# Rotary tables on GpSimd, latent masks as planned steps, a later second norm and a first copy on ScalarE in a three-part transformer kernel

## The chip, the cores and the metric

The kernel runs on one core of one Trainium2 chip. The metric is the device time of one launch in microseconds. A core has five engines with a queue each: TensorE (PE in the profile, its weight loads PEld), VectorE (DVE), ScalarE (ACT), GpSimd (POOL) and SyncE (SP), which here only issues DMAs. Each queue is worked off in the order in which the program put its instructions. An instruction that waits for another engine holds up what is queued behind it.

## The reference

The input x has 8 sequences of 512 tokens with 128 channels. Three blocks follow one another: a feed-forward stack at half weight, a causal attention with low-rank (latent) projections, and the same feed-forward stack again.

```
x = x + 0.5 * ffn(layernorm(x))
x = x + latent_attention(layernorm(x))     # 16 heads of 8, causal
x = x + 0.5 * ffn(layernorm(x))

ffn(x), for each of two layers l:
  h = shift_token(x)                       # half the channels come from the token before
  q, k, v = split(h @ wqkv[l])             # 8 heads of 64
  q = l2norm(q) * q_scale[l]; k = l2norm(k) * k_scale[l]
  q, k = rotary_xpos(q, k)
  x = x + local_attention(8 * q, k, v) @ wo[l]          # window of 64, one window back
  h = layernorm(shift_token(x)) * ln_g[l] + ln_b[l]
  a, g = split(h @ w1[l] + b1[l])
  x = x + (a * gelu(g)) @ w2[l] + b2[l]
```

All arithmetic is in float32, but for masks in bfloat16 that are added by products.

## The kernel before, in words

The program has three parts: `ffn("f0")`, `latent_attention()` and `ffn("f1")`. A feed-forward part goes over two layers and eight sequences (l, b), each sequence in four blocks of 128 tokens. A block is projected to q, k and v on TensorE (L542). ScalarE squares q and k (L568). DVE multiplies them by the rotary tables (c at L552, s at L555), GpSimd adds the two (L576) and later scales k (L612). Transposes (L504), scores (L675), a maximum on DVE (L684, L685), exponentials on ScalarE (L692), a division on GpSimd (L700), transposes of the probabilities, products with v (L758) and the output projection (L782) follow. After the fourth block comes the sequence's gated feed-forward (L849 to L902).

**The planner.** In the two `ffn` parts nobody writes the order of the instructions by hand. The code registers steps with a kind, an engine, a cost in microseconds and a rank, together with what they read and write. The rank is 100 times a position k (four per sequence, one per block) plus a number per kind from the table `PLACE`. `Plan.run` (L159 on) then keeps a clock for each engine. Again and again it takes the engine on which a step can begin first, and of its steps that can begin by then, the one of lowest rank. Only the first 110 steps by rank are looked at (`AHEAD`, L89). The order found so is fixed: it is the order of each queue on the chip. A change of one cost or rank can therefore reorder what comes after it.

**The head of the program.** Before the plan of f0, the code at L285 to L335 makes constants on GpSimd: the identity, two `band` masks for the local attention, and then three masks of the latent attention (`rows_of`, `causal`, `causal_t`; memsets at L317, selects at L325) and two rows of constants, `rows_sb` (L332). These stand ahead of all planned steps in GpSimd's queue, since they are not steps. The masks are first read by the masked products of the latent maxima (L1288), which the planner places near the end of f0; `rows_sb` is read by `fill_rows`, a DMA on SP.

**A sequence's beginning.** `shift(l, b, k)` begins a sequence. In layer 0 it has a norm in four steps: statistics on DVE (L484 to L486, kind "ist"), a logarithm and an exponential on ScalarE (L467, L468, "inr"), one Newton step on GpSimd (L471 to L474, "inn"), and the application on DVE (L492, "ina"). Then TensorE transposes ("sh"), and two copies fill hT: the first half of the channels on DVE (L520, "sd") and the half shifted by a token on ScalarE (L528, "sa").

**The rotary tables.** `rotary_table(l, s, ...)` (L344 on) multiplies the constant table by q_scale or k_scale of one layer. It is called four times (two layers, q and k), each time with three products, as steps of kind "tb" with rank `100 * 2 * l - 450`. Their inputs lie in the buffer `u` of the feed-forward. The latent weights use it next (loads at L984, products at L998, copies at L1004), and afterwards the feed-forward itself.

Of the kernel before, what the change touches and what calls it, by code (L numbers as in the profile page):

```python
# [16 lines left out]
P = 128  # L17
# [12 lines left out]
    "hs": 650, "hd": 390, "he": 330, "fst": 40, "fnr": -330, "fnn": 790, "fna": -289, "b2": 60,  # L30
    "ft": 620, "fc": 750, "g": 1010, "ge": 950, "a": 1, "u": 161, "po": 1030, "y2": 870,
    "ld": -1100, "lst": -900, "lnr": -880, "lnn": -870, "lna": -860, "lz": -1000, "lo": -990, "l3": -300, "l4": -290, "lt": -850, "lx": -840, "lq": -830, "lc": -820, "ls": -810, "lv": -700, "lu": -690, "lm": -600, "lr": -590, "lf": -400, "et": 0, "ed": 0, "ex": 0, "ev": 0, "es": 0, "ep": 0, "ee": 0,
    "lw": -400, "tb": -450, "fi": 990, "fo": 1230,
}


# [152 lines left out]
def kernel(  # L189
# [121 lines left out]
    def quadrant(g):  # L311
        return slice(32 * g, 32 * g + 32)

    masks = {}
    for name in ("rows_of", "causal", "causal_t"):
        masks[name] = const.tile([P, 4, P], BF16, name=name)
        nc.gpsimd.memset(masks[name], 0.0)  # L317
    for g in range(4):
        for name, pattern, sign, op, fill in (
            ("rows_of", [[-32, 4], [1, P]], -1, ALU.not_equal, 1.0),  # L320
            ("causal", [[32, 4], [-1, P]], 1, ALU.is_ge, MASKED),
            ("causal_t", [[-32, 4], [1, P]], -1, ALU.is_ge, MASKED),
        ):
            rows = masks[name][quadrant(g)]
            nc.gpsimd.affine_select(  # L325
                out=rows, in_=rows, pattern=pattern, compare_op=op, fill=fill, base=0,
                channel_multiplier=sign,
            )

    rows_sb = const.tile([4, 2, P], F32, name="rows_sb")  # L330
    for k in range(2):
        nc.gpsimd.memset(rows_sb[:, k], float(k))  # L332

    def fill_rows(dst, k):
        nc.sync.dma_start(  # L335
# [7 lines left out]

    def rotary_table(l, s, rot_sb, scales):  # L344
        t, g = tabs[l], scales[:, s, l]
        nc.vector.tensor_mul(
            t[:, 2 * s], rot_sb[:, 2 * s], g.unsqueeze(1).to_broadcast([P, NB, DH])
        )
        for lo, fr in ((0, HD), (HD, 0)):
            nc.vector.tensor_mul(  # L350
                t[:, 2 * s + 1, :, lo : lo + HD],
                rot_sb[:, 2 * s + 1, :, lo : lo + HD],
                g[:, fr : fr + HD].unsqueeze(1).to_broadcast([P, NB, HD]),
            )
# [53 lines left out]
    def ffn(tagname, last):  # L408
        plan = Plan(tc, nc)

        def step(kind, engine, cost, at, *args, **kw):
            return plan.step(kind, engine, cost, 100 * at + PLACE[kind], *args, **kw)
# [95 lines left out]
        def shift(l, b, k):  # L508

            y = [("Y", b, i) for i in range(NB)]  # L510
            if l == 0:
                norm(k, "i", lambda: X[:, b], lambda: Y[:, b], [("X", b)], y, [])
            tp, hT = Slot(mm), Slot(r_hT)
            half = C // 2
            step(
                "sh", PE, 0.5, k, lambda: transposes(lambda i: Y[:, b, i], tp),
                y + ([("W", l)] if l else []), [tp], [tp], 0.1,
            )
            step(
                "sd", DVE, 0.62, k, lambda: nc.vector.tensor_copy(hT[:half, :], tp[:half, :]),  # L520
                [tp], [(hT, 0)], [tp, hT], 0.1,
            )
            step(
                "sp", POOL, 0.1, k, lambda: nc.gpsimd.memset(hT[half:, 0:1], 0.0),
                [], [(hT, 1)], [hT],
            )
            step(
                "sa", ACT, 0.5, k, lambda: nc.scalar.copy(hT[half:, 1:T], tp[half:, 0 : T - 1]),  # L528
                [tp], [(hT, 2)], [tp, hT], 0.1,
            )  # L530
            seqs[l, b] = hT, Slot(r_kT), Slot(r_V2), Slot(r_V)
# [395 lines left out]
        def first_loads():  # L927

            tables_u = Slot(r_u)
            size = 4 * NB * DH  # L930

            def rotary():
                return flat(tables_u.tile)[:, :size].rearrange(
                    "p (f n d) -> p f n d", f=4, n=NB
                )

            def scales():
                return flat(tables_u.tile)[:, size : size + 2 * L * DH].rearrange(
                    "p (s l d) -> p s l d", s=2, l=L
                )  # L940

            for t, scale in enumerate((q_scale, k_scale)):
                load_step(
                    0, lambda t=t, scale=scale: nc.sync.dma_start(
                        out=scales()[:, t].rearrange("p l d -> p (l d)"),
                        in_=scale.rearrange("l d -> (l d)").partition_broadcast(P),
                    ), [tables_u], [tables_u],
                )
            load_step(0, lambda: nc.sync.dma_start(out=rotary(), in_=rot), [tables_u], [tables_u])
            for l in range(L):  # L950
                for t in range(2):
                    step(
                        "tb", DVE, 1.2, 2 * l,
                        lambda l=l, t=t: rotary_table(l, t, rotary(), scales()),
                        [tables_u], [("tab", l, t)], [tables_u],
                    )
            load_step(0, lambda: nc.sync.dma_start(out=cols_sb, in_=cols), [("W", 0)])
            for what in load_layer(0):
                load_step(1, what, [("W", 0)])
            for b in range(1, B):  # L960
                load_step(NB * b, lambda b=b: load_tokens(b), [("X", b)])
            load_step(
                NB * 3, lambda: nc.sync.dma_start(out=wqkv_sb[1], in_=wqkv[1]), [("W", 1)]
            )
            for what in load_layer(1):
                load_step(NB * 4, what, [("W", 1)])
            latent_weights()

        def latent_weights():

# [38 lines left out]
        def latent_begins():  # L1009
# [4 lines left out]
            for b in range(2):  # L1014
                q, kk, v = Slot(r_kT), Slot(r_V), Slot(r_V2)
                for name, t in (("q", q), ("k", kk), ("v", v)):
                    head_slots[name, b] = t
                    step(
                        "lz", POOL, 1.95, k, lambda t=t: nc.gpsimd.memset(t.tile, 0.0),
                        [], [t], [t], 0.0, [done[L - 1, B - 2 + b, NB - 1], done[L - 1, B - 1, 0]],  # L1020
                    )
                step("lo", SP, 0.55, k, lambda kk=kk: fill_rows(kk.tile, 1), [kk], [kk], [kk], 1.8)
                step(
                    "lz", POOL, 0.3, k,
                    lambda b=b: nc.gpsimd.memset(heads("v", b)[:, :, :, MD : MD + 1], 1.0),
                    [v], [v], [v],
                )
# [49 lines left out]
            for b, held in [(0, held) for held in MAXIMA] + [(1, held) for held in MAXIMA[:LEAD]]:  # L1077
                q, kk = head_slots["q", b], head_slots["k", b]
                m = maxima_of(b)
                for half in (0, 1):  # L1080
# [6 lines left out]
                        lambda b=b, held=held, units=units: by_turns(  # L1087
                            [maximum_products(b, held, g, bank) for g, bank in units]
                        ),
                        [(q, "d"), (kk, "d")], banks, [q, kk] + banks, 0.1,  # L1090
                    )
                    for (g, bank), t in zip(units, banks):
                        step(
# [530 lines left out]
```

## Time and profile before

| what | value |
|---|---|
| median of 3 runs | 1869.26 us (1868.18 to 1870.35) |
| the profiled execution, its own time | 1873.94 us |
| its span, first to last instruction | 1872.2 us |
| mean granted TensorE clock | 0.978 |
| first transposes on TensorE | 15.70 us |
| first projection on TensorE (L542) | 18.37 us |
| first gates of a feed-forward (table load before L855) | 138.9 us |
| first masked product of the latent maxima (L1288) | 773.9 us |
| first hT copy of the second half (L520) | 1133.17 us |

Times in the profile are microseconds from the first instruction. A timeline row gives start, duration, engine, line, operation and tiles. A bracket behind it names the idle time before the instruction and what ended that time. A row marked xN stands for N instructions in a row; then the duration is the stretch from the first start to the last end. In the rows of busy time by stretch, each engine's busy microseconds come with the number of its instructions, followed by the clock that TensorE was granted (1.00 is full) and the share of the time that the DMA engines were busy. The page's slices divide the span into 40 parts of 46.8 us; a digit is a share in tenths.

### The profile page before, as it was taken

How to read it: one execution, taken by the hardware profiler on the slowest of the kernel's cores; microseconds unless marked ns; L12 is line 12 of the kernel's file. 1: busy time of each engine (PE TensorE's matmuls, PEld its weight loads, DVE VectorE, ACT ScalarE, POOL GpSimd, SP SyncE). 2: the span in 40 equal slices, each digit the busy share in tenths (PEclk: the TensorE clock that was granted, in tenths of full speed). 3: DMA queues.
4: the chain of work that ended last, by engine and by line, in shares of the span. 5: the costliest groups of instructions: out<-in, count | busy, mean ns of one | idle time of the engine just before them, and what ended most of it. 6: DMA issues, size and time to landing. Idle time of an engine off the chain costs nothing.

```text
span 1872.2 us, 50913 instructions
## 1 busy us (share of the span) xinstructions
PE 1751.0 (94%) x19860; PEld 1178.7 (63%) x19860; DVE 1371.9 (73%) x2884; ACT 1391.0 (74%) x3911; POOL 988.0 (53%) x1685
## 2 busy tenths in 40 slices
PE   4999999999999999899999998999999999999998
PEld 2656666666666656477777764666666666666665
DVE  5878877777778777567767646878877777777764
ACT  2888888878888877227667666878888888788875
POOL 5776666666666666100000015867666666666651
PEclk8999999999999999769999999999999999999999
DMA  3211111111111111100000000111111111111110
GB/s 100 51 38 31 30 24 24 24 24 25 26 24 24 24 24 25 29 3 26 16 16 16 15 3 18 27 24 24 30 24 24 24 29 24 30 31 34 30 32 23
DMA packets 51968, 50.03 MB, mean 27 GB/s; under 512 B 22759, under 2 KB 34705, under 8 KB 51729
## 3 DMA queue, kind: packets, MB, share of 16 engines
q1 hardware_dynamic: 51584, 46.00, 10.6%
q8 instruction: 158, 2.59, 0.6%
q10 hardware_dynamic: 144, 0.79, 0.1%
q14 instruction: 82, 0.66, 0.1%
HBM read 6.30 MB, written 2.10 MB: 4 GB/s over the span
## 4 chain that ended last, share of the span: by engine, by line
PE 57%; DVE 18%; ACT 13%; POOL 7%; issue 4%; DMA 1%; SPq 1%; ACTq 0%; DVEq 0%; POOLq 0%
PE mm_f L542 10%; PE mm_f L504 8%; PE mm_f L849 6%; ACT pr_f L692 5%; PE mm_f L782 4%; PE st L1355 4%; PE sc L1297 4%; PE mm_f L891 4%; PE mm_f L758 4%; PE lo L1372 3%; DVE c_f L552 3%; DVE s_f L555 3%; PE sc_f L675 3%; ACT sq_f L568 3%; PE mm_f L1297 2%
## 5 line engine op out<-in xcount | busy, mean ns | idle before, releaser
L692 ACT ACTIVATE pr_f<-sc_f,nm_f,q_f 128x128 f32<-128x128 f32 x1024 | 458.0, 473 | 6.0 <-DVE nm_f L685 4.7
L542 PE MATMUL mm_f<-wqkv,hT_f 128*128 128x512 f32 x768 | 396.4, 621 | 30.8 <-DVE s_f L555 13.8
L576 POOL TENSOR_TENSOR qk_f<-c_f,s_f 128x512 f32<-128x512 f32 x256 | 324.7, 1273 | 118.8 <-DVE s_f L555 114.5
L700 POOL TENSOR_TENSOR pr_f<-pr_f,rso_f 128x512 f32<-128x512 f32 x256 | 265.8, 1039 | 219.1 <-DVE rso_f L716 185.0
L552 DVE TENSOR_TENSOR c_f<-mm_f,tab 128x512 f32<-128x512 f32 x256 | 175.1, 684 | 79.5 <-PE mm_f L542 35.1
L692 ACT ACTIVATION_READ_ACCUMULATOR pr_f<-sc_f,nm_f,q_f 128x1 f32 x1024 | 224.9, 220 | 0.0
L568 ACT ACTIVATE sq_f<-mm_f 128x512 f32<-128x512 f32 x256 | 153.3, 607 | 89.6 <-DVE s_f L555 60.8
L1366 ACT ACTIVATE pl<-st 128x512 f32<-128x512 f32 x280 | 156.2, 596 | 64.0 <-PE st L1355 54.8
L849 PE MATMUL mm_f<-fT_f,w 128*128 128x512 f32 (+1 forms) x384 | 191.7, 615 | 9.0 <-ACT ge_f L855 7.0
L504 PEld LDWEIGHTS mm_f<-ident,qk_f 128*128 128x128 f32 x1024 | 114.9, 142 | 125.3 <-POOL qk_f L612 49.7
L542 PEld LDWEIGHTS mm_f<-wqkv,hT_f 128*128 128x128 f32 x768 | 126.6, 195 | 103.0 <-issue 43.3
L684 DVE TENSOR_REDUCE nm_f<-sc_f 128x8 f32<-128x1024 f32 x128 | 155.2, 1213 | 45.2 <-PE sc_f L675 45.1
L504 PE MATMUL mm_f<-ident,qk_f 128*128 128x128 f32 x1024 | 160.3, 281 | 28.1 <-POOL qk_f L612 11.8
L758 PEld LDWEIGHTS mm_f<-pT_f,V_f 128*64 128x64 f32 (+1 forms) x4096 | 147.4, 136 | 60.2 <-issue 15.3
L758 PE MATMUL mm_f<-pT_f,V_f 128*64 128x64 f32 (+1 forms) x4096 | 179.8, 230 | 0.7 <-ACT pT_f L738 0.7
L555 DVE TENSOR_TENSOR s_f<-mm_f,tab 128x512 f32<-128x512 f32 x256 | 173.8, 679 | 0.0
L1387 POOL TENSOR_TENSOR X<-X,lon 128x128 f32<-128x128 f32 x27 | 11.9, 456 | 299.7 <-DVE lon L1381 299.4
L504 PE MATMUL mm_f<-ident,pr_f 128*128 128x128 f32 x1024 | 155.9, 279 | 11.8 <-DVE u_f L880 3.0
L504 PEld LDWEIGHTS mm_f<-ident,pr_f 128*128 128x128 f32 x1024 | 116.1, 142 | 74.5 <-POOL pr_f L700 32.7
L600 DVE TENSOR_REDUCE rn_f<-sq_f 128x16 f32<-128x1024 f32 x128 | 153.6, 1200 | 7.4 <-ACT sq_f L568 7.4
L782 PEld LDWEIGHTS mm_f<-wo,oT_f 128*128 128x128 f32 x1024 | 127.7, 191 | 43.1 <-ACT oT_f L771 18.2
L782 PE MATMUL mm_f<-wo,oT_f 128*128 128x128 f32 x1024 | 140.7, 280 | 3.3 <-ACT oT_f L771 2.9
(166 smaller groups left out, 3861.1 us busy)
## 6 DMA issues: line engine op xcount, KB each, us to landing
V_f<-V_f SPq DMA_DIRECT2D x224, 128.0 KB
hs_f<-Y SPq DMA_DIRECT2D x32, 112.0 KB
X<-in_x_dram SPq DMA_DIRECT2D x8, 256.0 KB
out_dram<-hs_f SPq DMA_DIRECT2D x8, 256.0 KB
Y<-fl SPq DMA_DIRECT2D x32, 32.0 KB
kT_f<-fl SPq DMA_DIRECT2D x32, 32.0 KB
V_f<-fl SPq DMA_DIRECT2D x32, 32.0 KB
wqkv<-in_wqkv_dram ACTq DMA_DIRECT2D x1, 768.0 KB
```

Of the source, the lines that this page charges most:

```text
L504: nc.tensor.transpose(dst[:, i * P : (i + 1) * P], src(i), ident)
L542: nc.tensor.matmul(ps.tile, lhsT=hT[:, i * P : (i + 1) * P], rhs=wqkv_sb[l][:, at * INNER : (at + 1) * INNER], start=True, stop=True,)
L552: nc.vector.tensor_mul(c1.tile, psv, tabs[l][:, 2 * s, i].unsqueeze(1).to_broadcast([P, H, DH]))
L555: nc.vector.tensor_mul(s1.tile.rearrange("p h (t d) -> p h t d", t=2), psv.rearrange("p h (t d) -> p h t d", t=2)[:, :, ::-1], tabs[l][:, ...
L568: lambda s=s, ps=ps: nc.scalar.activation(sq[:, s], ps.tile, AF.Square),
L576: lambda s=s, c1=c1, s1=s1: nc.gpsimd.tensor_add(qk[:, s].rearrange("p (h d) -> p h d", d=DH), c1.tile, s1.tile),
L692: nc.scalar.activation(pr[:, h], sv[:, h % 2, h // 2], AF.Exp, bias=nm[:, h % 2, h // 2 : h // 2 + 1], scale=q8[:, h : h + 1], accum_out=s ...
L700: nc.gpsimd.tensor_mul(pr[:, heads], pr[:, heads], inv[:, heads].unsqueeze(2).to_broadcast([P, H // 2, P]),)
L758: nc.tensor.matmul(o[r * DH : (r + 1) * DH, u * P + w * WIN : u * P + (w + 1) * WIN], lhsT=(V2, V)[w][keys, i, h * DH : (h + 1) * DH], rhs ...
L782: nc.tensor.matmul(pw[:, :C], lhsT=oT[:, pr], rhs=wo_sb[l][:, pr], start=(pr == 0), stop=(pr == INNER // P - 1),)
L849: nc.tensor.matmul(ps[: hsz[c], :], lhsT=w1_sb[l][:, at + c * P : at + c * P + hsz[c]], rhs=fT.tile, start=True, stop=True,)
L1366: nc.scalar.activation(dst, bank, AF.Exp, scale=MSCALE)
```

## The change

It has five edits.

1. The masks and rows at the head become a generator, `mask_parts`. Each of its 17 instructions is a step of its own on GpSimd: kind "lb", cost 0.65, position 5, so rank 500. The steps that read them get "masks" among their reads.
2. `rotary_table` uses GpSimd in place of DVE. Its steps are on POOL with cost 1.3, and their position is 4l in place of 2l.
3. The norm of sequence 1 in layer 0 gets position k + 2 in place of k, so 200 more in rank. That holds in f0 and in f1.
4. The copy "sd" of sequence 0 in layer 0 is done by ScalarE in place of DVE, with the planner's cost left at 0.62. That too holds in both halves.
5. `PLACE` gets an entry for "lb".

```
-    masks = {}
-    for name in ("rows_of", "causal", "causal_t"):
-        masks[name] = const.tile([P, 4, P], BF16, name=name)
-        nc.gpsimd.memset(masks[name], 0.0)
-    for g in range(4):
-        for name, pattern, sign, op, fill in (
...
+    def mask_parts():
+
+        for name, pattern, sign, op, fill in MASKS:
+            yield lambda name=name: nc.gpsimd.memset(masks[name], 0.0)
+            for g in range(4):
+                rows = masks[name][quadrant(g)]
+                yield lambda rows=rows, pattern=pattern, sign=sign, op=op, fill=fill: (
+                    nc.gpsimd.affine_select(
...
+        for k in range(2):
+            yield lambda k=k: nc.gpsimd.memset(rows_sb[:, k], float(k))
...
-        nc.vector.tensor_mul(
+        nc.gpsimd.tensor_mul(
             t[:, 2 * s], rot_sb[:, 2 * s], g.unsqueeze(1).to_broadcast([P, NB, DH])
         )
         for lo, fr in ((0, HD), (HD, 0)):
-            nc.vector.tensor_mul(
+            nc.gpsimd.tensor_mul(
...
             if l == 0:
-                norm(k, "i", lambda: X[:, b], lambda: Y[:, b], [("X", b)], y, [])
+
+                at = k + 2 if b == 1 else k
+                norm(at, "i", lambda: X[:, b], lambda: Y[:, b], [("X", b)], y, [])
...
             step(
-                "sd", DVE, 0.62, k, lambda: nc.vector.tensor_copy(hT[:half, :], tp[:half, :]),
+                "sd", DVE if l or b else ACT, 0.62, k,
+                lambda: (nc.vector.tensor_copy if l or b else nc.scalar.copy)(
+                    hT[:half, :], tp[:half, :]
+                ),
                 [tp], [(hT, 0)], [tp, hT], 0.1,
             )
...
-                        "tb", DVE, 1.2, 2 * l,
-                        lambda l=l, t=t: rotary_table(l, t, rotary(), scales()),
+                        "tb", POOL, 1.3, 4 * l,
+                        lambda l=l, t=t: rotary_table(
+                            l, t, rotary(), scales()
+                        ),
...
             latent_weights()
+            for what in mask_parts():
+                step("lb", POOL, 0.65, 5, what, [], ["masks"])
...
-                step("lo", SP, 0.55, k, lambda kk=kk: fill_rows(kk.tile, 1), [kk], [kk], [kk], 1.8)
+                step(
+                    "lo", SP, 0.55, k, lambda kk=kk: fill_rows(kk.tile, 1), [kk, "masks"], [kk],
+                    [kk], 1.8,
+                )
...
-                        [(q, "d"), (kk, "d")], banks, [q, kk] + banks, 0.1,
+                        [(q, "d"), (kk, "d"), "masks"], banks, [q, kk] + banks, 0.1,
```

## The prediction

> **What bounds the kernel now.** I read the page first, for the engine shares and the slices, since the edits touch a few microseconds of a 1872 us program and the question is whether their stage is bound by something else.
>
> ```profile
> PE 1751.0 (94%) x19860; PEld 1178.7 (63%) x19860; DVE 1371.9 (73%) x2884; ACT 1391.0 (74%) x3911; POOL 988.0 (53%) x1685
> ...
> PE   4999999999999999899999998999999999999998
> ...
> POOL 5776666666666666100000015867666666666651
> ```
>
> TensorE is the bound (94%) everywhere but in the first slice of 46.8 us, where its digit is 4. Time saved in that slice moves all later TensorE work forward, because little after it waits for anything but TensorE. So I took the first stretch apart in the timeline (start, duration, engine, line, operation):
>
> ```profile
> 4.68 0.52 POOL L317 MEMSET rows_of<- 128x512 bf16 x1
> ...
> 8.30 0.20 ACT L468 ACTIVATE ns_f<-ns_f 128x4 f32<-128x4 f32 x1
> ...
> 12.92 0.63 POOL L325 TENSOR_SCALAR_AFFINE_SELECT causal_t<-causal_t 32x512 bf16<-32x512 bf16 x1
> 13.61 0.34 POOL L332 MEMSET rows_sb<- 4x128 f32 x2
> 14.00 0.14 POOL L524 MEMSET hT_f<- 64x1 f32 x2
> 14.22 0.20 POOL L471 TENSOR_TENSOR nt_f<-ns_f 128x4 f32<-128x4 f32 x1
> ...
> 15.29 1.12 DVE L492 TENSOR_SCALAR Y<-X,mv_f,ns_f 128x128 f32<-128x128 f32 x4 [7.27 <-POOL ns_f L474]
> 15.69 0.95 PEld L504 LDWEIGHTS mm_f<-ident,Y 128*128 128x128 f32 x4 [15.69 <-DVE Y L492]
> ```
>
> The input of the first norm's Newton step (L471) is ready at 8.50, when ScalarE ends L468. GpSimd reaches that step only at 14.22, after the mask instructions from 4.68 to 13.95. DVE idles 7.27 us for it, and TensorE starts at 15.69. The DMA answer for 0 to 6 us shows the queue of the first weights finished (0.26 MB up to 3, 0.53 MB from 3 to 6; the tensor has 768 KB), so weights don't hold an earlier start.
>
> Then busy time by stretch (us, then PE, PEld, DVE, ACT, POOL, granted clock, DMA share, GB/s):
>
> ```profile
> 16.00:35.00 19.00, 13.01 (x26) 5.52 (x26) 14.67 (x39) 4.54 (x9) 7.26 (x9) 0.90 0.01 5
> 35.00:55.00 20.00, 16.48 (x115) 8.62 (x115) 16.92 (x37) 11.63 (x38) 13.03 (x25) 0.75 0.18 41
> 55.00:80.00 25.00, 23.73 (x253) 15.80 (x251) 20.45 (x45) 21.49 (x74) 18.16 (x33) 0.93 0.23 62
> ...
> 90.00:112.00 22.00, 20.48 (x237) 13.66 (x235) 17.70 (x38) 17.80 (x58) 18.16 (x38) 1.00 0.22 50
> ```
>
> From 16 to 55 TensorE lacks 9.5 us of work; from 25 to 40 DVE is busy 13.9 of 15 us, so there DVE leads. From 55 on TensorE is 95% busy. GpSimd has its fullest stretch at 90 to 112.
>
> **The change, part by part.** The sum is made against the profiled execution: span 1872.2, its own time 1873.94; the runs' median, 1869.26, is 4.7 lower, and I subtract the same amount from it.
>
> *Masks out of the head.* 17 instructions (3 memsets of 0.52, 12 selects of 0.63, 2 row memsets) leave GpSimd's queue ahead of the Newton step. That step then starts when L468's result arrives, 8.58 (a later pair in the trace, 27.86+0.20 to 28.14, shows 0.08 between them), not at 14.22: **-5.6 us**. X lands at 6.1 in either case, so no more is to be had here.
>
> *Rotary tables on GpSimd.* Each of four steps is three products of two SBUF operands: on DVE 0.42+0.49, 0.9 us. GpSimd's nearest rows are L612 and L700, 128x512 in 1.04: half that size twice over gives 1.04, some 1.2 with three starts. The Trainium skill (GPSIMD Engine Reference, "Engine selection") speaks against the move: such elementwise work belongs on VectorE, GpSimd being about twice as slow. By that rule four steps are 4 x 1.8 = 7.3 us, by the row 4.8. The rotary input should have landed by 9 to 10 (q1 had moved 0.90 MB at 9.0; inputs up to it are 0.93 MB). From 9.6 the first table ends at 10.8 by the row, 11.4 by the rule; all four at 14.4 or 16.9. Their cover is the transposes, the copies of hT and the first projection: the first reader (L552) ran at 21.08 and would be at 15.5, and GpSimd's first add (L576) at 16.8. By the row nothing is exposed; by the rule 0.1 us. I take the row: 0. Without that cover, a late input for instance, each microsecond stalls GpSimd's queue and the projection of q behind it.
>
> The same page's "Key points" warn that GpSimd shares its SBUF interfaces with VectorE. Here the trace has a price: the four L492 of sequence 0 took 1.12 us with GpSimd idle; those of sequence 1 ran beside L576:
>
> ```profile
> 29.13 2.49 POOL L576 TENSOR_TENSOR qk_f<-c_f,s_f 128x512 f32<-128x512 f32 x2
> ...
> 29.90 2.31 DVE L492 TENSOR_SCALAR Y<-X,mv_f,ns_f 128x128 f32<-128x128 f32 x4
> ```
>
> The moved products will run just when sequence 0's L492 do (9.65 to 10.8). Free of contention that is 0, fully contended 2.31-1.12 = 1.2. The products are shorter than the add, so I take half: **+0.6**.
>
> Off DVE: three of the four tables ran in idle time at 16 to 20. The fourth stood at 33.34 in the DVE-led stretch: between 0 and 0.9, I take **-0.7**. The latent weights wait for the tables' buffer, so their seven loads may be issued some 15 us sooner than 34.18. SP had nothing queued then but the second wqkv, and waits for nothing there.
>
> *Second norm further back.* Statistics (25.70 to 27.59) and L492 (29.90 to 32.21) take 4.2 us of DVE's time while projections of sequence 0 wait for it. They are postponed, not removed, and TensorE's projections of sequence 1, its filler at 33.5, come later with them. Between -4.2 (DVE later has 15% slack in the TensorE-bound part) and +3 (filler missing for as long as TensorE idled at 27.0 to 30.1). I take **-1.5**. In the second half these steps run at 1104 to 1107 with DVE mostly idle: 0 there; if they slid into 1135 to 1160, 3.0 us of DVE time would stand in a DVE-led stretch.
>
> *First copy on ScalarE.* Both copies of hT already run one after the other (16.98+0.58, then 17.59+0.68); 0.58 for 0.68 and no change of engine: -0.1. In the second half 0.68 us leaves DVE at 1133. ScalarE has nothing queued behind at the start; in the second half exponentials follow it. From -0.8 to +0.6: **-0.3** in all.
>
> *Masks as steps.* Some 9.8 us of GpSimd work come back with rank 500. The plan looks 110 steps ahead; by my count about 270 steps have a lower rank (37 for each of the first four blocks, parts of the next, loads, latent weights), so the masks appear after about 160, that is around 60 to 110 us. GpSimd is 73% busy there (18.16 of 25), 83% at 90 to 112. A step caught behind one waits up to 0.63 us, and TensorE through it only if no other chain is ready. From 0 (all in gaps) to 9.8 (all on the path); nearer the first, as TensorE has several chains open: **+1.0**. The added waits (L1288's products, the row fill on SP) are met 650 us early: nothing is queued behind them that sees it. Should those 650 us vanish, the first products would stand up to 9.8 us.
>
> *The order of everything else.* The planner is greedy; other costs and ranks reshuffle both halves. Rows give a scale only: TensorE's busy time in the 100-us stretches of 240 to 640 lies between 94.8 and 96.1, say 0.65 each; over twelve such stretches 0.65 x 3.5 = 2.3 us, and the ends of both halves (TensorE's wait of 4.3 us for ScalarE at 770, the tail) may move as much again. I take 0, within 4 either way.
>
> Sum: -5.6+0.6-0.7-1.5-0.3+1.0 = **-6.5**: 1873.94 becomes 1867.4, and the median 1862.8.
>
> **Rivals.** *The start is given back* (1868): TensorE starts 5.0 sooner, but DVE, which leads from 25 to 40, gives nothing more (the 2.5 of the table, norm and copy stay out), and masks and order cost 4. For it: DVE's 13.9 of 15 us. Against: DVE's chain starts sooner as well. *More is won* (1857): the postponed norm counts in full (2.7 more), the masks lie in gaps (1.0), and the order gives 2. For it: TensorE's gap at 27 to 30 would close, and with it perhaps the low clock. The page has 0.50 granted from 32 to 44; weight loads are 0.85 apart at 20 to 24 as at 41 to 43, so TensorE was slow all along, whatever the column says before 30. The Trainium skill (TensorE: Matmul & The Clock Gate, "HAM oscillation — how this bites in real kernels") asks for no idle gaps above some 3.4 us. By that rule the gap here, 3.1, lowers nothing and closing it frees nothing; by the row the clock fell right after it, and closing it could free up to half of the 12 us that TensorE was busy from 30 to 45. DVE leads there, so I give it 0. *Slower* (1874): the masks land on the path. Their place is 90 to 112, where GpSimd has 3.8 of 22 us free: 9.8 us more can't fit, the quotients of the probabilities (L700) come late, and TensorE idles for each piece. With the other gains lost this is -5.0+9.8 = +4.8. It decides once 8.7 of the 9.8 us are on the path; that other chains were open in this stretch (TensorE 93% busy) speaks against it. *The change doesn't do what it says*: the planner might draw the masks to the front again, into GpSimd's idle head; then start and time stay as before, 1869. The rank and the look-ahead speak against it.
>
> **How the numbers follow.** Two runs of this kernel can be told apart at about 0.2%, 3.7 us; so faster means under 1865.5, slower over 1873. Main case (1858 to 1867): 0.55, of which 0.03 over 1865.5. More won: 0.15. Given back, or not done (1865.5 to 1873): 0.16. Slower: 0.14. Faster 0.52+0.15 = 0.67; same 0.03+0.16 = 0.19; slower 0.14. The range 1854 to 1873 leaves out the rival above and some 0.04 below.
>
> **What would show it.** The Newton step at 8.5 to 9 and the first transposes near 10.3, not 15.7; table products on GpSimd between 9.5 and 15, none on DVE; L492 of sequence 0 between 1.1 and 2.3; first projection near 13; TensorE busy over 26 of the first 47 us (23.4 now); selects on GpSimd only after 50. I am wrong if the first transposes come sooner by 5 us but the first feed-forward's gates, at 139 now, don't; or if the latent stage, first masked products at 773.9, starts late; or if the second half, from 1133 to the end, grows by more than 3 us.

## The result and the profile after

| what | before | after |
|---|---|---|
| median of the runs taken in turn on one chip (4 each) | 1868.72 us | 1885.20 us (1881.88 to 1887.19) |
| ratio of the runs, 95% interval | | 1.0086 [1.0074, 1.0098] |
| span of the profiled execution | 1872.2 us | 1883.3 us |
| mean granted clock | 0.978 | 0.980 |
| first transposes on TensorE | 15.70 us | 10.08 us |
| first gates of the first half | 138.9 us | 137.4 us |
| first masked product of the latent maxima | 773.9 us | 772.0 us |
| last products of the latent stage | 1097.2 us | 1095.0 us |
| from there to the end of the span | 775.0 us | 788.3 us |

The change made the kernel 16.5 us slower; a gain of 6.5 us was forecast. The start came out as forecast. The other end of the table holds the loss: the second half, in which only two of the five edits act, is 13.3 us longer.

The diff shifts the line numbers. What was L492 (the norm's application) is L496, L504 (transposes) L508, L542 (projection) L551, L555 (second rotary product) L564, L576 (the add on GpSimd) L585, L700 (the quotient) L709, L325 and L332 (masks, rows) L330 and L336. Experiments built nearer to the old text have numbers between.

The rows of the page after that answer to those of before, the first for the engine totals and the others for the 40 slices:

```profile
PE 1750.9 (93%) x19860; PEld 1178.9 (63%) x19860; DVE 1370.2 (73%) x2870; ACT 1390.7 (74%) x3913; POOL 996.1 (53%) x1697
...
PE   6799999999999989799999998889999999999998
...
POOL 6776766666666665100000006756666666666651
```

TensorE does the same 1750.9 us of work (1751.0 before), so the added time is idle time of TensorE. Its first digit rose from 4 to 6 and its second fell from 9 to 7: what the head won, the next slice gave back. Behind the latent stage two more slices show an 8 where they showed a 9.

The start in the timeline of the changed kernel (start, duration, engine, line, operation; in brackets the idle time ahead and what ended it):

```profile
8.61 0.20 POOL L475 TENSOR_TENSOR nt_f<-ns_f 128x4 f32<-128x4 f32 x1 [3.92 <-ACT ns_f L472]
...
9.68 1.60 DVE L496 TENSOR_SCALAR Y<-X,mv_f,ns_f 128x128 f32<-128x128 f32 x4 [1.70 <-POOL ns_f L478]
...
10.08 0.99 PE L508 MATMUL mm_f<-ident,Y 128*128 128x128 f32 x3 [10.08 <-DVE Y L496]
10.47 0.72 POOL L350 TENSOR_TENSOR tab<-u_f 128x256 f32<-128x256 f32 x1 [0.83 <-DMA u_f<-in_rot_dram]
...
11.98 0.73 POOL L350 TENSOR_TENSOR tab<-u_f 128x256 f32<-128x256 f32 x1
```

The Newton step starts at 8.61 in place of 14.22, and the transposes come 5.6 us sooner. The tables run on GpSimd, one every 1.5 us, while the transposes and copies of sequence 0 proceed.

Busy time by stretch (us; then PE, PEld, DVE, ACT, POOL; granted clock, DMA share, GB/s), first the changed kernel:

```profile
0.00:47.00 47.00, 29.80 (x196) 16.02 (x200) 32.27 (x77) 22.95 (x69) 32.54 (x75) 0.96 0.37 111
47.00:140.00 93.00, 77.94 (x841) 50.78 (x842) 72.66 (x153) 67.76 (x216) 71.81 (x121) 0.98 0.16 39
1140.00:1200.00 60.00, 49.88 (x541) 31.80 (x540) 49.31 (x92) 45.00 (x148) 45.14 (x80) 0.97 0.12 28
1200.00:1300.00 100.00, 88.65 (x862) 57.65 (x862) 78.80 (x174) 76.77 (x236) 66.05 (x111) 0.97 0.11 25
```

and the kernel before:

```profile
0.00:47.00 47.00, 23.39 (x50) 9.84 (x50) 27.15 (x72) 11.46 (x26) 26.97 (x64) 0.85 0.34 100
47.00:140.00 93.00, 85.65 (x938) 56.47 (x942) 75.76 (x162) 76.69 (x255) 69.45 (x118) 0.98 0.18 43
1140.00:1200.00 60.00, 52.87 (x528) 32.80 (x530) 53.00 (x98) 46.37 (x152) 49.49 (x82) 0.97 0.12 26
1200.00:1300.00 100.00, 93.95 (x994) 63.77 (x994) 83.03 (x182) 82.77 (x256) 69.20 (x122) 0.98 0.12 27
```

In the first 47 us TensorE is busy 6.4 us more than before, from 47 to 140 it is busy 7.7 us less. From 1140 to 1300 it is busy 8.3 us less (3.0 and 5.3).

One caution for all marks of the first half: the profiled execution of the kernel before had a low clock (0.79 on average from 20 to 60), and eight experiments below that leave the first half as it was (e6, e8, e9, e10, e13, e14, e17, e18) reached the last latent products at 1092.5 to 1095.0, not 1097.2, and the first gates at 135.8 to 137.0, with a clock of 0.87 to 0.91. Against those the changed kernel's 1095.0 and 137.4 are no gain at all.

### The profile page after: what moved, and what is told of

It reads as the page before. It is cut to its first block, busy times and chain, and to the rows that moved or that the text cites. A ratio compares the mean times of both kernels' runs of the same rounds, so it can differ in the third digit from the quotient of the medians.

```text
span 1883.3 us, 50901 instructions
## 1 busy us (share of the span) xinstructions
PE 1750.9 (93%) x19860; PEld 1178.9 (63%) x19860; DVE 1370.2 (73%) x2870; ACT 1390.7 (74%) x3913; POOL 996.1 (53%) x1697
## 4 chain that ended last, share of the span: by engine, by line
PE 55%; DVE 19%; ACT 15%; POOL 5%; issue 4%; DMA 1%; SPq 1%; ACTq 0%; DVEq 0%; POOLq 0%
PE mm_f L551 8%; PE mm_f L508 8%; ACT pr_f L701 6%; PE mm_f L858 5%; PE mm_f L900 4%; PE mm_f L767 4%; PE st L1371 4%; DVE c_f L561 4%; PE sc L1313 3%; PE mm_f L791 3%; PE lo L1388 3%; DVE s_f L564 3%; PE sc_f L684 3%; ACT sq_f L577 3%; DVE nm_f L693 2%
## 5 line engine op out<-in xcount | busy, mean ns | idle before, releaser
L551 PE MATMUL mm_f<-wqkv,hT_f 128*128 128x512 f32 x768 | 390.6, 612 | 37.3 <-DVE s_f L564 14.8
L585 POOL TENSOR_TENSOR qk_f<-c_f,s_f 128x512 f32<-128x512 f32 x256 | 326.7, 1280 | 129.0 <-DVE s_f L564 105.8
L709 POOL TENSOR_TENSOR pr_f<-pr_f,rso_f 128x512 f32<-128x512 f32 x256 | 265.9, 1040 | 197.3 <-DVE rso_f L725 167.9
L508 PEld LDWEIGHTS mm_f<-ident,qk_f 128*128 128x128 f32 x1024 | 114.3, 142 | 131.1 <-POOL qk_f L621 54.5
L551 PEld LDWEIGHTS mm_f<-wqkv,hT_f 128*128 128x128 f32 x768 | 124.8, 192 | 109.7 <-issue 42.4
L508 PE MATMUL mm_f<-ident,qk_f 128*128 128x128 f32 x1024 | 161.4, 281 | 33.4 <-POOL qk_f L621 13.5
L564 DVE TENSOR_TENSOR s_f<-mm_f,tab 128x512 f32<-128x512 f32 x256 | 173.7, 679 | 0.0
L508 PE MATMUL mm_f<-ident,pr_f 128*128 128x128 f32 x1024 | 156.1, 280 | 14.8 <-DVE s_f L564 2.1
L508 PEld LDWEIGHTS mm_f<-ident,pr_f 128*128 128x128 f32 x1024 | 116.4, 142 | 82.2 <-issue 34.9
```

Of the source, the lines that this page charges most:

```text
L508: nc.tensor.transpose(dst[:, i * P : (i + 1) * P], src(i), ident)
L551: nc.tensor.matmul(ps.tile, lhsT=hT[:, i * P : (i + 1) * P], rhs=wqkv_sb[l][:, at * INNER : (at + 1) * INNER], start=True, stop=True,)
L564: nc.vector.tensor_mul(s1.tile.rearrange("p h (t d) -> p h t d", t=2), psv.rearrange("p h (t d) -> p h t d", t=2)[:, :, ::-1], tabs[l][:, ...
L585: lambda s=s, c1=c1, s1=s1: nc.gpsimd.tensor_add(qk[:, s].rearrange("p (h d) -> p h d", d=DH), c1.tile, s1.tile),
L709: nc.gpsimd.tensor_mul(pr[:, heads], pr[:, heads], inv[:, heads].unsqueeze(2).to_broadcast([P, H // 2, P]),)
```

## The experiments

Each was timed in turn with the kernel before on the same chip. Differences in us are between the two medians taken together; the ratio with its 95% interval decides.

### In which half the time is lost

All edits in f0 alone, with f1 as before, and the reverse. `last` is true in the second half.

```
  # e5: first half alone, masks as steps and tables on GpSimd as in the change
- at = k + 2 if b == 1 else k
+ at = k + 2 if b == 1 and not last else k
- "sd", DVE if l or b else ACT, 0.62, k,
+ "sd", DVE if l or b or last else ACT, 0.62, k,
  # e6: second half alone, masks at the head and tables on DVE as before
- at = k + 2 if b == 1 else k
+ at = k + 2 if b == 1 and last else k
- "sd", DVE if l or b else ACT, 0.62, k,
+ "sd", ACT if not (l or b) and last else DVE, 0.62, k,
```

> All edits of the first half (masks, tables, later norm, copy), the second half as before. If the loss lies in the second half alone: as the changed kernel's first half showed, -1 to -4 us against before, about 1868. If the first half loses as well (masks on the path at 80 to 90): within 2 us of before or over it.

> The first half as before; the second half with the later norm and the copy on ScalarE, whose order on every engine equals the changed kernel's there. Theory A2 (the order that the plan finds for these two edits together costs): 786 to 789 us from the last value products of the latent stage to the end, 775 before; total +11 to +14, about 1883. If it was a disturbance that reached the second half from the first: within 3 us of before.

Measured: first half 1869.62 against 1868.50, 1.0010 [1.0002, 1.0019]; second half 1882.02 against 1868.50, 1.0074 [1.0058, 1.0091]. So +1.1 us where -6.5 was forecast, and +13.5 where nothing was. The masks and tables can't be the cause of most of the loss: the second kernel has neither as steps.

### One edit at a time, in both halves

Each on the kernel before, with the lines of the change:

```
  # e1: later norm
+ at = k + 2 if b == 1 else k
  # e2: copy
- "sd", DVE, 0.62, k, lambda: nc.vector.tensor_copy(hT[:half, :], tp[:half, :]),
+ "sd", DVE if l or b else ACT, 0.62, k,
  # e3: masks as steps
+ step("lb", POOL, 0.65, 5, what, [], ["masks"])
  # e4: tables
- "tb", DVE, 1.2, 2 * l,
+ "tb", POOL, 1.3, 4 * l,
```

> The kernel before with the later second norm alone, in both halves. Theory A (the postponed norm takes sequence 1's projections from TensorE as filler): about 1882 us, 12 to 15 over before, nearly all between the end of the latent stage and the end (775.0 us from the last value products to the end now, 786 to 789 then); in the first half +1 to +4. Theory B (the masks are what costs): within 2 us of before. Theory C (any edit reshuffles the plan by several us either way): anything from -5 to +15, and the other single edits as far off as this one.

> The kernel before with the first copy on ScalarE alone, in both halves; the second half's order on TensorE stays as before. Theory A: -1 to +1 us. A rival for the second half (the copy that ScalarE now does ahead of the first squares is what costs 13 us): +8 to +13. Theory C: several us either way in spite of the equal order.

> The kernel before with the masks as planned steps alone. First transposes near 10.1 in place of 15.7 in any case. Theory A with masks on the path: the start gains 5.6, and most of it is given back where the masks stand in GpSimd's queue (70 to 90 us): first feed-forward's gates 0 to 3 us sooner than 138.9, total -3 to +1 us. Masks hidden: -5.6. Theory C: between -5 and +8.

> The kernel before with the rotary tables on GpSimd alone, the masks still at the head. The tables then follow the Newton step on GpSimd at 15.3 and take 6.2 us (1.55 each, as in the changed kernel): the first add on GpSimd waits until 21.5 and is not late. Theory A: -1 to +1.5 us. Theory C: several us either way.

| edit alone | us against before | ratio |
|---|---|---|
| `at = k + 2 if b == 1` (later norm) | +7.7 | 1.0043 [1.0028, 1.0058] |
| "sd" of sequence 0 on ScalarE | -2.2 | 0.9987 [0.9980, 0.9995] |
| masks as steps, position 5 | -4.9 | 0.9973 [0.9966, 0.9981] |
| tables on GpSimd, position 4l | -1.4 | 0.9994 [0.9986, 1.0002] |

Only the later norm loses. The four add up to -0.8; together they make +16.5, so more than 17 us come from their meeting. The norm's +7.7 is below the 12 to 15 of my theory A, and the copy's -2.2 lies outside its -1 to +1. The copy alone leaves the order of the second half on TensorE and GpSimd exactly as before.

### The later norm taken away, alone, and in other sizes

```
  # e7, on the changed kernel
- at = k + 2 if b == 1 else k
+ at = k
  # e8, on the kernel before
+ at = k + 2 if b == 1 and last else k
  # e9 and e10, on e6
- at = k + 2 if b == 1 and last else k
+ at = k + 3 if b == 1 and last else k
+ at = k + 1 if b == 1 and last else k
```

> The changed kernel with the second norm back at its old position in both halves. Theory A2: the second half as before (775 us), the first half 5 to 7 us shorter: 1862 to 1866. If the copy on ScalarE or the masks carry the loss: over 1872.

> Only the second half's norm is later, nothing else. If missing filler is the whole cause, whatever the order after it: +11 to +13. Theory A2 (it takes the copy too to tip the order): 0 to +4, second half 775 to 779 us.

> The kernel before with the copy on ScalarE and the norm of the second half's sequence 1 three positions later in place of two (600 against 300 and 200 in rank: 3 where the change has 2). Sequence 1's transposes come about 20 TensorE rows later still than in the changed kernel, but from sequence 2 on the plan returns to the rows it has with the norm alone. If missing filler is the cause, the loss grows with the delay: +13 or more, 788 us and over from the last latent value products to the end. If it is the order that the plan happens to find (theory A2): +2 to +6, as with the norm alone, 777 to 781.

> As the run before, with the norm one position later. Sequence 1's transposes move by 17 TensorE rows only (70 in the changed kernel). Missing filler: 0 to +3. Theory A2: another order again, -2 to +6.

| kernel | us against before | ratio |
|---|---|---|
| e7, changed kernel without the later norm | -0.7 | 0.9993 [0.9984, 1.0002] |
| e8, later norm alone, second half | +3.9 | 1.0023 [1.0016, 1.0030] |
| e10, copy, norm one position later | +0.2 | 1.0005 [0.9998, 1.0012] |
| e6, copy, norm two positions later | +13.5 | 1.0074 [1.0058, 1.0091] |
| e9, copy, norm three positions later | +5.6 | 1.0036 [1.0017, 1.0055] |

Without the later norm the changed kernel is level with the kernel before (the interval of e7 holds 1), yet it doesn't win what it should: my -5 to -7 was missed. One, two and three positions cost 0, 13.5 and 5.6 us: the loss doesn't grow with the delay. My theory until then, "DVE work and the filler are postponed into a full stretch" with a price per microsecond of delay, falls here; in its place came the order that the planner makes.

### Where the masks go in the first half

In the changed kernel the masks came at 70 to 89. The timeline of that stretch, of the changed kernel:

```profile
78.31 0.68 DVE L564 TENSOR_TENSOR s_f<-mm_f,tab 128x512 f32<-128x512 f32 x1
...
80.24 0.63 POOL L330 TENSOR_SCALAR_AFFINE_SELECT rows_of<-rows_of 32x512 bf16<-32x512 bf16 x1
...
81.53 2.66 POOL L330 TENSOR_SCALAR_AFFINE_SELECT causal<-causal 32x512 bf16<-32x512 bf16 x4
...
85.85 2.65 POOL L330 TENSOR_SCALAR_AFFINE_SELECT causal_t<-causal_t 32x512 bf16<-32x512 bf16 x4
...
88.98 1.27 POOL L585 TENSOR_TENSOR qk_f<-c_f,s_f 128x512 f32<-128x512 f32 x1
...
90.31 1.11 PE L508 MATMUL mm_f<-ident,qk_f 128*128 128x128 f32 x4 [2.84 <-POOL qk_f L585]
```

The add L585 has its inputs at 78.99, when DVE ends L564. It runs at 88.98, behind the masks (7.3 of these 10 us) and two other instructions, and TensorE idles 2.84 us for it. From 80 to 90 TensorE is busy 6.40 of 10 us (8.73 before). So the masks were not all in gaps. The next four kernels move them elsewhere.

```
- step("lb", POOL, 0.65, 5, what, [], ["masks"])
  # e11: tables on GpSimd, copy on ScalarE in f0, no later norm
  # e12: tables on DVE, copy on ScalarE in f0 and f1, no later norm
+ step("lb", POOL, 0.65, 5 + 1 * n, what, [], ["masks"])      # n-th mask step
  # e15: all else as before
  # e16: tables on GpSimd, copy on ScalarE in f0, all else as before
+ step("lb", POOL, 0.65, 40, what, [], ["masks"])
```

> Masks, tables and copy in the first half as changed, norm as before, and the 17 mask steps one position apart each (rank 500, 600, 700 and so on), so that GpSimd gets one per block over some 300 us in place of all within 20 us; the second half as before. If the masks' crowding at 70 to 90 us is what eats the first half's gain: 5 to 8 us under before, about 1862. If not: as with the masks together, within 2 us of before.

> The masks as steps one position apart and the copy on ScalarE in both halves, tables on DVE, norm as before. If crowding was the cost: 5 to 8 us under before. Against the run with the tables on GpSimd it tells what the tables are worth: within 2 us if they are hidden, 3 or more under it if they disturb.

> The kernel before with the masks as steps at position 40 in place of 5, nothing else. TensorE's order is the old one through the first 1213 rows; only the masks are gone from the head. If the start's 5.6 us carry through the stretch that DVE leads: -5 to -6. If DVE takes part of it back: -2 to -3. As against the masks at position 5 (5 under before): lower by more than 2 if the crowding there costs.

> As the run before with the tables on GpSimd and the copy on ScalarE too in the first half. If those two are harmless: within 1.5 us of the run before. If they are what takes the start's gain (as the run of masks, tables and copy without the norm suggests, 0.7 under before): 3 to 5 us over the run before, within 2 of the kernel before.

| kernel | us against before | ratio |
|---|---|---|
| e11, masks spread | -2.6 | 0.9995 [0.9985, 1.0005] |
| e12, masks spread, no tables | -0.7 | 0.9999 [0.9990, 1.0009] |
| e15, masks at position 40 | -4.2 | 0.9977 [0.9968, 0.9986] |
| e16, the same, tables and copy | -6.0 | 0.9967 [0.9954, 0.9980] |

The two medians of e11 are 2.6 us apart, but by the ratio e11 can't be told from the kernel before. Spread out, the masks no longer crowd 70 to 100 (TensorE busy 27.66 of 30 us in e11, 23.10 in the changed kernel, 26.33 before). From 100 to 140 TensorE was then busy 35.98 of 40 (37.93 before), in another order and with a granted clock of 0.91 (1.00 before); which of the two counts there isn't shown. At position 40, the masks reach GpSimd at about 456 us (the view of the tile `causal`, of e16):

```profile
L330 POOL TENSOR_SCALAR_AFFINE_SELECT causal<-causal x4: 626/628/633, 456.7 to 458.9; 32x512 bf16<-32x512 bf16 x4
```

There the start's gain is kept, and tables and copy take nothing from it: e16 lies 1.8 us under e15, which their overlapping intervals don't tell apart. The busy time by stretch of e16, in the columns used above:

```profile
0.00:47.00 47.00, 28.73 (x142) 13.96 (x142) 31.48 (x72) 16.73 (x43) 29.85 (x73) 0.85 0.39 105
47.00:140.00 93.00, 83.39 (x923) 56.71 (x924) 75.48 (x167) 79.33 (x260) 68.81 (x113) 1.00 0.17 42
```

TensorE has been busy 112.1 us by 140 with 1065 recorded matmuls, against 107.7 us and 1037 in the changed kernel, and the first gates run at 131.4. e16 has the lowest median of the study and is faster than the kernel before and the changed one; e3 and e15 can't be told from it.

### What the second half loses: delay or order

The start of each feed-forward shows as a table load on ScalarE, so the distance from one sequence's first gates to the next can be read off. In e6 these loads stand at

```profile
1246.07 1.28 ACT L860 ACT_TABLE_LOAD   x1
...
1292.07 1.28 ACT L860 ACT_TABLE_LOAD   x1
...
1336.25 1.28 ACT L860 ACT_TABLE_LOAD   x1
```

so its distances are 46.0 and 44.2. Counted from the last latent products (1093.25 in e6; us):

| kernel | first gates | to the second | to the third | whole loss by the runs |
|---|---|---|---|---|
| before | 145.9 | 44.2 | 42.3 | 0 |
| e6, changed second half | 152.8 | 46.0 | 44.2 | +13.5 |
| e8, later norm alone | 151.1 | 42.3 | 42.3 | +3.9 |
| e9, three positions | 153.9 | 42.6 | 42.3 | +5.6 |

The changed second half loses twice: 6.9 us up to the first gates, then 3.7 more in two steps. Afterwards it keeps pace. This is 10.6 us in one execution, 3 short of the 13.5 that the runs show for e6; in the changed kernel's own trace, with the same order, the first gates come at 155.0 and the steps are 45.9 and 44.2. The first column goes with the granted clock too. Ten kernels have TensorE's old order in the second half: e3, e5, e15 and e16 have their first gates at 144.2 to 144.3, and the clock is 1.00 from 1137 to 1234; the other six, the kernel before among them, at 145.5 to 146.1, with 0.96. The two steps are 44.2 and 42.3 in all ten. So the first column is good to about 2 us, and the steps are the firmer mark.

e8 and e9 lose at the start too, but not in the steps. In the order of TensorE's instructions they differ from e6, among other things, in where sequences 4 and 5 are begun: at rows 472 and 596 of TensorE's order in the second half, not 472 and 622 (before: 498 and 596). The traces show the same in matmuls since the half's first transposes: 1178 and 1614, not 1178 and 1662 (before: 1226 and 1614). Four kernels move only the third sequence (number 2):

```
+ at += -0.5 if b == 2 and last else 0    # e13, on e6
+ at += 2 if b == 2 and last else 0       # e14, on the kernel before
+ at += -1 if b == 2 and last else 0      # e17, on e6
+ at += 1 if b == 2 and last else 0       # e18, on the kernel before
```

> The second half as in the changed kernel (later norm of sequence 1, copy on ScalarE; first half as before), and there sequence 2's norm half a position earlier, so that its transposes move from 282 to 219 TensorE rows into the half (before: 259), with sequences 3, 4 and 5 at the changed kernel's rows. Theory A3 (TensorE is short of filler twice, since the order starts both sequence 1 and sequence 2 late): most of the loss behind the first feed-forward goes: +3 to +7 against before, 778 to 782 us from the last latent value products. If the loss belongs to the whole order or to sequence 1 alone: still +10 to +14.

> The kernel before with sequence 2's norm in the second half two positions later: its transposes at 305 TensorE rows in place of 259, sequence 1's as before. Theory A3: +3 to +7 from this delay alone. If only sequence 1's delay costs: within 2 us of before. If the later rows (sequences 4 and 5, which stand as in the changed kernel here) carry the loss: +8 or more.

> The first half as before; the second half with the later norm and the copy as in the changed kernel, but the norm of sequence 2 a whole position earlier. Theory A: the 13.5 us of the changed second half are two losses. One is the start, until the first gates of the second half (6.9 us there). The other, 3.7, falls between the first and the third gates (distances 46.0 and 44.2 where the kernel before has 44.2 and 42.3), in the kernels whose later sequences 4 and 5 have their transposes at TensorE rows 472 and 622, and not in those with 472 and 596 (42.3 and 42.3, a gain of 1.9). This kernel has 472 and 596 and its sequence 2 as early as the run with half a position has it (first gates 2.2 late there): so distances of 42.3 and 42.3, first gates 2 to 5 late, and in all 0 to +4 us against the kernel before. Theory B: the loss lies with sequence 1's late norm and its copy, whatever the later rows are: +8 to +13. Theory C: only where sequence 2 begins counts: earlier than in the run with half a position, by one row, so the same +8.

> The kernel before with the norm of sequence 2 one position later in the second half (two positions cost 8.5 us, 3.0 of it up to the first gates and 3.5 between first and third gates). Sequences 4 and 5 stand at TensorE rows 498 and 596, as in the kernel before. Theory A (start and later rows are two losses): distances between gates of 44.2 and 42.3 as before, and 0 to 3 us for the start; in all 0 to +3. Theory B and C (the place of sequence 2 alone): about half of the 8.5, +3 to +5, with part of it between the gates.

| kernel | first gates | to the second | to the third | us against before | ratio |
|---|---|---|---|---|---|
| e13 | 148.2 | 45.9 | 44.2 | +8.7 | 1.0049 [1.0032, 1.0066] |
| e14 | 148.9 | 45.8 | 44.2 | +8.5 | 1.0049 [1.0031, 1.0068] |
| e17 | 147.7 | 42.3 | 42.3 | +0.4 | 1.0002 [0.9992, 1.0012] |
| e18 | 148.0 | 44.2 | 42.3 | +2.7 | 1.0012 [1.0003, 1.0021] |

e17 decides. It has the later norm of sequence 1 and the copy on ScalarE, as the changed second half has, and all its work; only the rank of one other norm is 100 lower. The 13.5 us are gone, and its loads stand 42.3 apart:

```profile
1241.25 1.28 ACT L861 ACT_TABLE_LOAD   x1
...
1283.55 1.28 ACT L861 ACT_TABLE_LOAD   x1
...
1325.85 1.28 ACT L861 ACT_TABLE_LOAD   x1
```

e14 makes 8.5 us of loss with neither edit. So the loss isn't the price of the two edits' instructions, but of the order that the planner finds with them. In e17 the steps and the total went as the theory of two losses had it, and the start lost 1.8, just under its 2 to 5. In e18 steps, start and total went so too, but the interval of its total, 0.6 to 3.9 us, reaches into the +3 to +5 of the rivals; there the steps alone speak against them. e13, at +8.7, fell between both of its forecasts. In all nine kernels looked at, the distances go with the rows at which sequences 4 and 5 are begun: 46 and 44 with 472 and 622 (e6, e13, e14), 44 and 42 with 498 and 596 (before, e10, e18), 42 and 42 with 472 and 596 (e8, e9, e17). The changed kernel goes with e6, and e1 with e8.

The waits of TensorE from first to third gates (who was waited for, us in total, times, longest), in the changed kernel, 1250 to 1340:

```profile
PE mm_f L858 <- ACT ge_f L864: 1.2, 2, 0.6
PE mm_f L508 <- DVE s_f L564: 0.8, 1, 0.8
PE mm_f L791 <- DVE hT_f L527: 0.6, 1, 0.6
PE mm_f L508 <- POOL qk_f L621: 0.6, 1, 0.6
PE mm_f L551 <- ACT sq_f L577: 0.6, 2, 0.3
PE mm_f L508 <- DVE u_f L889: 0.4, 1, 0.4
PE mm_f L551 <- ACT V_f L593: 0.3, 1, 0.3
```

and the same view of e17, 1241 to 1326:

```profile
PE mm_f L548 <- ACT pr_f L698: 0.4, 2, 0.2
```

Nearly the same work (879 matmuls and 876) has nine waits of 4.5 us in the one order, spread over ScalarE, DVE and GpSimd, and two of 0.4 in the other. No single instruction is to blame in the first.

## Why the prediction was wrong

**Right, by its own signs.** The Newton step at 8.61, the first transposes at 10.08, the first projection at 13.11, TensorE busy 29.80 us of the first 47, tables on GpSimd from 10.47 on, selects only from 70 on: *masks out of the head* is worth its 5.6 us at the start. The contention term was forecast at +0.6: the four applications took 1.60 beside the table products, 1.12 alone, so +0.5 (three of them took 0.34 each, the one that ran beside the first product 0.83). A table step takes 1.50 us (10.47 to 11.98), between the 1.2 of the row taken and the 1.8 of the rule; the first c at 15.28 came behind the first table's end at 12.03, so nothing was exposed. (The trace names a table as what ended TensorE's 1.31 us of idle time ahead of the projection at 13.11, but the projection reads hT, and ScalarE's copy into it ended at 13.02.) Tables, copy and start together are -5.6+0.6-0.7-0.3 = -6.0 in the sum; e16, which has these with the masks far off and the copy in the first half alone, measured -6.0. Its interval runs from -8.6 to -3.7, so that the two numbers agree to the tenth is luck.

**One reading was wrong.** TensorE wasn't "slow all along": in the kernel before its weight loads are 0.85 apart from 20.21 to 23.63, but 0.43 from 24.42 to 24.85, ahead of the gap, and 0.85 again at 41 to 43, behind it. The rule of 3.4 us that the prediction set beside this gap doesn't hold here: the clock fell behind a gap of 3.1, and in e16 at 22.8 us behind one of 1.9. The price of 0 put on closing the gap has no run of its own.

**The step that failed: *second norm further back*, and in it "in the second half these steps run at 1104 to 1107 with DVE mostly idle: 0 there".** The later norm alone, in the second half alone, costs +3.9 (e8); with the copy beside it, which alone costs nothing (e2), +13.5 (e6). The step priced the moved instructions where they stood, and took it that nothing else would be placed anew. The timeline of TensorE in the kernel before shows what was taken away: the transposes of sequences 0 and 1 stood together, eight in a row.

```profile
1132.48 1.09 PE L504 MATMUL mm_f<-ident,Y 128*128 128x128 f32 x8
```

The same view of the changed kernel has four, and the next four much later:

```profile
1130.26 0.66 PE L508 MATMUL mm_f<-ident,Y 128*128 128x128 f32 x4
...
1160.14 0.60 PE L508 MATMUL mm_f<-ident,Y 128*128 128x128 f32 x4
```

Sequence 1, TensorE's filler while the chain of sequence 0 goes round the other engines, is ready 28 us later. The step itself had the case ("if they slid into 1135 to 1160, 3.0 us of DVE time would stand in a DVE-led stretch") and gave it no price in the sum: the application did slide, to 1156.40. Even so 3.0 us would have been short by 10.

**And *the order of everything else*, 0 within 4.** That bound came from the spread of TensorE's busy time over stretches of one order; it says how even a given order is, not what another order may cost. Shifting a single norm by one position or two moved the time by 13 us (e6 to e17) and 8.5 us (e14). This is the mis-sized bound behind a range that ended at 1873: the 9.6 us between e8 and e6 alone are more than twice its 4.

**First half: -6.5 forecast, +1.1 measured (e5).** *Masks as steps* was +1.0. From e16 to e7, which differ in the masks' place (and in the second half's copy, which leaves the order there alone), lie 5.3 us by the runs. This fits the rival "slower", masks on the path, though at 80 to 90 rather than at 90 to 112, and not at the full 9.8. It isn't a price of the place alone: without tables and copy (the masks alone, -4.9; e15, -4.2) position 5 costs nothing, and spreading them out (e11) cures the crowding without winning the time in the runs. *Second norm further back* in f0 was -1.5: e5 is 1.8 worse than e7, and the later norm in both halves (+7.7) is 3.8 worse than in the second alone (e8).

In one sum: -6.0 for start, tables and copy, +5.3 for the masks' place, +1.8 for the later norm in f0 (these three are e5's +1.1, cut up by the runs), +13.5 for the second half, together +14.6 of the 16.5 measured. The 1.9 that are left lie within the intervals.

**The marks that were to prove me wrong** did so: the first gates came at 137.4 and not 5 us sooner than 138.9, and the second half grew by 13.3 us, over 3. The latent stage wasn't late.

**What stays open.** Why the planner's choice differs, step by step, wasn't followed: which engine's clock in the plan tips it. Which of the two, sequences 4 and 5 begun at rows 472 and 622 or something that comes with it, makes the steps 46 and 44 us long, is a correlation over nine kernels, not shown apart. And in the first half, crowding on GpSimd and changed order weren't separated in e7. The traces don't even place the 5.3 us there: e16 has its first gates 4.2 us ahead of e7 (131.4 and 135.6), but the last latent products only 0.8 (1088.8 and 1089.6); the rest of the lead between these two executions lies in the second half (771.3 and 775.1 us), where TensorE's order is the same. Single profiled executions differ from the medians by up to 5 us (the kernel before: 1873.94 and 1868.72), so a finer split isn't to be had from them.

## What to carry to other kernels

Where a greedy planner fixes the order, an edit has two prices: that of its instructions, which the rows give, and that of the order that the new costs and ranks lead to. The second was up to 13.5 us here and showed no trend with the size of the edit, so a sum from the rows needs a range of that size for every half in which an edit touches a rank. Before an edit of that kind is given up, move a neighbour's rank by one position: e17 got the 13.5 us back that way, though no more than that. And one place is not as good as another for work that no one needs for 650 us: out of the head, position 5 cost nothing alone (e3) but lost the gain beside tables and copy (e7), while position 40 kept it in both (e15, e16).

## What the runs showed of the hardware

- The table product of 128x256 float32 took 0.73 us on GpSimd and 0.42 on DVE, 1.7 times as long. GpSimd's add, 128x512 from two DVE products, took 1.27, the quotient of the same size 1.04.
- Four norm applications on DVE (1.12 us alone) took 1.60 beside GpSimd's table products, with the whole delay in one of the four (0.83 in place of 0.34), and 2.31 beside its adds.
- Where the granted clock was lower at the start of the second half, its first gates came about 1.5 us later, in the same order on TensorE: 144.2 to 144.3 us behind the last latent products at 1.00 (four kernels), 145.5 to 146.1 at 0.96 (six kernels).
- The clock column is not a full account of TensorE's speed. In the changed kernel the weight loads of the first projections start 0.86 us apart from 14.10 to 18.37 and 0.43 apart from 18.93 to 20.22, while the column shows 1.00 from 8 to 20.
- A lower column in one stretch does not rank two kernels of different order. From 16 to 35 us it shows 1.00 in the changed kernel and 0.68 in e16, and e16 has its first gates 6 us sooner (131.4 against 137.4).
